# Counting relation ids as base-128 digits and batching the half-row operand products in a two-layer graph kernel

**Chip, cores, metric.** One core of one Trainium2 chip. The metric is the device time of one execution in microseconds (us), as the median of several executions. The core's span in a profile is some 2 us shorter than that time.

## The reference, cut to what matters

128 graphs of 64 nodes with 768 features, `adj` holding 0 or 1. Layer 0 is a relational graph layer in which `adj` serves both as adjacency and as relation ids; layer 1 is a gated attention layer that the change doesn't touch.

```python
h = relu(layernorm(x))                       # layer 0
ctx = (adj @ (h @ Wadj.T + badj)) / deg + (adj.T @ (h @ Wrev.T + brev)) / rdeg + h @ Wself.T + bself
agg  = einsum('bij,bijr->bir', adj, E[rels])             # rels is adj
ragg = einsum('bij,bijr->bir', adj.T, E[rels.T + 40])
x = x + ctx + agg @ Wr.T + ragg @ Wrr.T + bias terms
# layer 1 works on relu(layernorm(x)) and doesn't take part in the argument
```

Because only an id's count matters, the kernel counts for every node how often each of the ids 1 to 39 occurs in its row and in its column, and multiplies the counts with a table of 39 + 39 + 3 rows.

## The kernel before

The kernel has two stages, one for each layer. A stage walks over 32 pairs of tiles of 128 rows (two graphs a tile). In the first stage, TensorE computes the seven products of a Strassen-like scheme for a pair, in 67 steps; the preparation of the next pair is merged into these steps at stated positions:

```python
def count(p, k, d):                    # on VectorE, four times a pair
    eq = work.tile([P, NV, N], BF16, name="eq", bufs=1)
    nc.vector.tensor_tensor(eq, AB[p][:, k, d, None, :].to_broadcast([P, NV, N]), vals, op=OP.is_equal)
    nc.vector.tensor_reduce(CNT[p][:, k, d * NV : (d + 1) * NV], eq, AX.X, OP.add)
    ...
def operands(p, k, q):                 # on TensorE, six times a pair
    ps = pss.tile([P, GT, 512], F32, name="pb")          # two such PSUM buffers
    for i in range(2):
        for g in range(GT):            # one graph: 64 of the 128 rows
            s = slice(g * N, (g + 1) * N)
            nc.tensor.matmul(ps[:, g, i * 3 * N : (i + 1) * 3 * N], H0[t][s, kb * P : (kb + 1) * P],
                             rts[p % 2][s, k]..., start=True, stop=True)
    if k == 0:                         # evicted by ScalarE
        nc.scalar.copy(A1[p][:, q]..., pv); return
    nc.scalar.copy(A22..., pv[:, :, 3:])
    nc.vector.tensor_sub(S3..., A1..., pv[:, :, :3])     # evicted by VectorE
    nc.vector.tensor_add(S1..., A22..., pv[:, :, :3])    # S1 has one buffer
...
steps = [..., (10, lambda: count(p, 0, 0)), (15, lambda: count(p, 0, 1)), (39, lambda: sum2(p)),
         (44, lambda: count(p, 1, 0)), (49, lambda: count(p, 1, 1)),
         (46, lambda: count_t(p, 0)), (62, lambda: count_t(p, 1)), ...]
for q in range(KH):                    # KH = 3
    steps.append((20 + 3 * q, lambda q=q: operands(p, 0, q)))
    steps.append((30 + 4 * q, lambda q=q: operands(p, 1, q)))
```

The position sets an instruction's priority. The framework that builds the program fixes the order on each engine ahead of time, by its own estimate of what is ready when; an instruction with a late position may still be placed early, where the estimate sees its engine idle.

Of the kernel before, what the change touches and what calls it, by code (L numbers as in the profile page):

```python
# [8 lines left out]
F32 = mybir.dt.float32  # L9
BF16 = mybir.dt.bfloat16  # L10
I32 = mybir.dt.int32
AF = mybir.ActivationFunctionType
OP = mybir.AluOpType
AX = mybir.AxisListType

P = 128
# [6 lines left out]
def kernel(  # L23
# [48 lines left out]
    nc = tc.nc  # L72
    G, N, D = x.shape
    NREL = e_t.shape[1]
    NB = NREL // 2
    NV = NB - 1
    KB = D // P
    KH = KB // 2
# [4 lines left out]
    NP = NT // 2  # L83
    HALF = D // 2
    HH = H // 2
    NCNT = 2 * NV


    NROW = NCNT + 3
    PARTS = ((0, P // 3), (P // 3, NROW))  # L90
    W = DO + 1
    assert GT == 2 and N == 64 and DO == P and H == KB and KB % 2 == 0 and H % 2 == 0
    assert 3 * (NROW - P // 3) <= P and NT % 2 == 0 and HALF <= 512 and HH * W <= 512

# [57 lines left out]
    with ExitStack() as px:  # L152
        wa = px.enter_context(tc.tile_pool(name="wa", bufs=1))
        work = px.enter_context(tc.tile_pool(name="work0", bufs=2))
# [5 lines left out]
        def load(p):  # L160
            if p >= NP:
                return
            for t in (2 * p, 2 * p + 1):
                X[t] = work.tile([P, D], F32, name="x", bufs=6)
                nc.sync.dma_start(X[t], xf[t * P : (t + 1) * P, :])
            AI[p] = work.tile([P, 2, 2, N], I32, name="ai")
            for d, src in ((0, adj), (1, adj_t)):
                nc.sync.dma_start(
                    AI[p][:, :, d, :],
                    src[p * 2 * GT : (p + 1) * 2 * GT].rearrange("(t g) i j -> (g i) t j", g=GT))  # L170
# [23 lines left out]
        for i, v in enumerate((br, brr, badj, brev, bself)):  # L194
# [6 lines left out]
        blkb = wa.tile([P, P], BF16, name="blkb")  # L201
        nc.vector.tensor_copy(blkb, blk)

        vals = wa.tile([P, NV, N], BF16, name="vals")
        nc.gpsimd.iota(vals, pattern=[[1, NV], [0, N]], base=1, channel_multiplier=0,
                       allow_small_or_imprecise_dtypes=True)
        rts = []
        for i in range(2):
# [58 lines left out]
                                                   op0=OP.mult, op1=OP.add)  # L267
                nc.vector.tensor_copy(tab, u[:m])

        H0, ADF, AB, CNT, CT_T = {}, {}, {}, {}, {}  # L270
        A1, A22, S1, S2, S3, S4 = {}, {}, {}, {}, {}, {}

        def norm(t):
            to = small.tile([P, 2], F32, name="rn")
            stats(X[t], to)
            h = H0[t] = work.tile([P, D], F32, name="h0")
            nc.scalar.activation(h, X[t], AF.Relu, scale=to[:, 0:1], bias=to[:, 1:2])  # L277

        def prep(p):

            af = ADF[p] = work.tile([P, 2, 2, N], F32, name="af", bufs=1)
            nc.vector.tensor_copy(af, AI[p])
            AB[p] = work.tile([P, 2, 2, N], BF16, name="ab")
            nc.gpsimd.tensor_copy(AB[p], af)  # L284
            cnt = CNT[p] = work.tile([P, 2, NROW], BF16, name="cnt")
            dg = small.tile([P, 2, 2], F32, name="dg")
            nc.vector.tensor_reduce(dg, af, AX.X, OP.add)
            nc.vector.tensor_scalar(cnt[:, :, NCNT : NCNT + 2], dg, 1.0, None, op0=OP.min)
            nc.vector.memset(cnt[:, :, NCNT + 2 : NCNT + 3], 1.0)

        def prep_r(p):


            ds = pss.tile([P, 2, 512], F32, name="pb")[:, 0, : 4 * N].rearrange(
                "p (k d n) -> p k d n", k=2, d=2)
            nc.tensor.matmul(ds, blkb, AB[p], start=True, stop=True)
            rd = work.tile([P, 2, 2, N], F32, name="rd", bufs=1)
            nc.vector.tensor_scalar(rd, ds, 1.0, None, op0=OP.max)
            nc.vector.reciprocal(rd, rd)
            for d in range(2):  # L300
                nc.vector.tensor_mul(rts[p % 2][:, :, 1 - d, :], ADF[p][:, :, d, :], rd[:, :, d, :])

        def count(p, k, d):
            eq = work.tile([P, NV, N], BF16, name="eq", bufs=1)
            nc.vector.tensor_tensor(  # L305
                eq, AB[p][:, k, d, None, :].to_broadcast([P, NV, N]), vals, op=OP.is_equal)
            with nc.allow_low_precision(reason="whole numbers up to 64"):
                nc.vector.tensor_reduce(CNT[p][:, k, d * NV : (d + 1) * NV], eq, AX.X, OP.add)  # L308
            if d == 1:
                c3 = CT_T[p, k] = work.tile([P, NROW, 3], BF16, name="c3")  # L310
                nc.gpsimd.tensor_copy(c3, CNT[p][:, k, :, None].to_broadcast([P, NROW, 3]))

        def count_t(p, k):
            c3 = CT_T[p, k]
            pn = pss.tile([P, 2, 512], F32, name="pb")[:, 0, :P].bitcast(BF16).rearrange(
                "p (i n) -> p i n", i=2)
            cn = CT_T[p, k] = work.tile([P, 2, P], BF16, name="cntT", bufs=4)
            for i, (a, b) in enumerate(PARTS):
                nc.tensor.transpose(pn[: 3 * (b - a), i, :],  # L319
                                    c3[:, a:b, :].rearrange("p v c -> p (v c)"), identb)  # L320
                nc.scalar.copy(cn[: 3 * (b - a), i, :], pn[: 3 * (b - a), i, :])  # L321

        def operands(p, k, q):


            t = 2 * p + k
            ps = pss.tile([P, GT, 512], F32, name="pb")
            for i in range(2):
                kb = 2 * q + i
                for g in range(GT):  # L330
                    s = slice(g * N, (g + 1) * N)
                    nc.tensor.matmul(ps[:, g, i * 3 * N : (i + 1) * 3 * N],  # L332
                                     H0[t][s, kb * P : (kb + 1) * P],
                                     rts[p % 2][s, k].rearrange("p s n -> p (s n)"),
                                     start=True, stop=True)
            pv = ps[:, :, : 6 * N].rearrange("p g (x n) -> p g x n", n=N)

            def blocks(ap):
                return ap.rearrange("p s (g n) -> p g s n", g=GT)

            if k == 0:
                if q == 0:
                    A1[p] = work.tile([P, KH, 2, 3, P], F32, name="a1")
                nc.scalar.copy(A1[p][:, q].rearrange("p h s (g n) -> p g (h s) n", g=GT), pv)  # L344
                return
            if q == 0:
                A22[p] = work.tile([P, KH, 3, P], F32, name="a22")
                S1[p] = work.tile([P, KH, 3, P], F32, name="s1", bufs=1)
                S3[p] = work.tile([P, KH, 3, P], F32, name="s3")
            nc.scalar.copy(blocks(A22[p][:, q]), pv[:, :, 3:])  # L350
            nc.vector.tensor_sub(blocks(S3[p][:, q]), blocks(A1[p][:, q, 0]), pv[:, :, :3])
            nc.vector.tensor_add(blocks(S1[p][:, q]), blocks(A22[p][:, q]), pv[:, :, :3])

        def sum2(p):
            S2[p] = work.tile([P, KH, 3, P], F32, name="s2", bufs=1)
            for q in range(KH):
                nc.gpsimd.tensor_sub(S2[p][:, q], S1[p][:, q], A1[p][:, q, 0])  # L357

        def sum4(p):
            S4[p] = work.tile([P, KH, 3, P], F32, name="s4", bufs=1)  # L360
            for q in range(KH):
                nc.gpsimd.tensor_sub(S4[p][:, q], A1[p][:, q, 1], S2[p][:, q])
# [68 lines left out]
        def side(p):  # L431

            if p >= NP:
                return []
            steps = [(4, lambda: load(p + 1)),
                     (0, lambda: prep(p)),
                     (0, lambda: norm(2 * p)),
                     (0, lambda: norm(2 * p + 1)),
                     (6, lambda: prep_r(p)),
                     (10, lambda: count(p, 0, 0)),  # L440
                     (15, lambda: count(p, 0, 1)),
                     (39, lambda: sum2(p)),
                     (44, lambda: count(p, 1, 0)),
                     (49, lambda: count(p, 1, 1)),
                     (46, lambda: count_t(p, 0)),
                     (62, lambda: count_t(p, 1)),
                     (99, lambda: sum4(p))]
            for q in range(KH):
                steps.append((20 + 3 * q, lambda q=q: operands(p, 0, q)))
                steps.append((30 + 4 * q, lambda q=q: operands(p, 1, q)))  # L450
            return steps

        def sums_of_weights():
            for q in range(KH):
# [20 lines left out]
    with ExitStack() as px:  # L475
        wb = px.enter_context(tc.tile_pool(name="wb", bufs=1))
        work = px.enter_context(tc.tile_pool(name="work1", bufs=2))
# [84 lines left out]
        def main(p):  # L562
# [19 lines left out]
            def part(t, s, q):  # L582
                if s == 0:
                    return HS[t][:, q * HH : (q + 1) * HH, :DO]
                return Z[t][:, q * HALF : (q + 1) * HALF].rearrange("p (h o) -> p h o", h=HH)

# [230 lines left out]
```

## Time and profile before

| | before |
|---|---|
| time, median of 3 | 2788.27 us (2785.63 to 2789.57) |
| start, to 126 us | TensorE 61% busy |
| steady part of the first stage, 126 to 1617 us | TensorE 100%, VectorE 66% busy |
| one pair in the steady part | 48.75 us |

A row of the profile's groups reads: source line, engine, operation, output<-input names, shapes, number of instructions | busy us, mean ns of one | idle time of the engine just before them and what ended most of it. PE is TensorE, PEld its weight loader, DVE VectorE, ACT ScalarE, POOL GpSimd.

### The profile page before, as it was taken

How to read it: one execution, taken by the hardware profiler on the slowest of the kernel's cores; microseconds unless marked ns; L12 is line 12 of the kernel's file. 1: busy time of each engine (PE TensorE's matmuls, PEld its weight loads, DVE VectorE, ACT ScalarE, POOL GpSimd, SP SyncE). 2: the span in 40 equal slices, each digit the busy share in tenths (PEclk: the TensorE clock that was granted, in tenths of full speed). 3: DMA queues.
4: the chain of work that ended last, by engine and by line, in shares of the span. 5: the costliest groups of instructions: out<-in, count | busy, mean ns of one | idle time of the engine just before them, and what ended most of it. 6: DMA issues, size and time to landing. Idle time of an engine off the chain costs nothing.

```text
span 2786.5 us, 29364 instructions
## 1 busy us (share of the span) xinstructions
PE 2677.9 (96%) x10360; PEld 1605.5 (58%) x10360; DVE 2013.0 (72%) x3928; ACT 857.1 (31%) x1891; POOL 667.6 (24%) x703
## 2 busy tenths in 40 slices
PE   3999999999999999999999969999999999999996
PEld 2555555555555555555555536666666666666663
DVE  8975757667675766757576227888888888888887
ACT  1111112111111211111121104555555555555554
POOL 4422223232222323222222212111111111112220
PEclk8999999999999999999999989999999999999998
DMA  4111112121111212111120141222222222222211
GB/s 155 38 37 43 65 36 72 36 72 36 44 65 37 72 36 72 36 45 64 36 70 35 46 179 36 70 70 70 71 70 70 70 71 70 70 72 75 72 57 40
DMA packets 90596, 173.07 MB, mean 62 GB/s; under 512 B 32845, under 2 KB 40653, under 8 KB 90450
## 3 DMA queue, kind: packets, MB, share of 16 engines
q1 hardware_dynamic: 81432, 157.32, 16.8%
q10 hardware_dynamic: 9018, 13.89, 1.4%
q8 instruction: 82, 1.34, 0.2%
q14 instruction: 64, 0.52, 0.1%
HBM read 95.67 MB, written 75.50 MB: 61 GB/s over the span
## 4 chain that ended last, share of the span: by engine, by line
PE 72%; DVE 17%; ACT 6%; issue 3%; DMA 2%; POOL 0%; SPq 0%; ACTq 0%; DVEq 0%; POOLq 0%
PE pwa L376 20%; PE pwb L376 14%; PE pwd L376 7%; PE pwc L376 6%; PE pb L332 6%; PE pma L573 5%; PE pmc L573 5%; DVE no L651 4%; PE pmb L573 2%; DVE f L721 2%; ACT e L720 2%; DVE f L722 2%; DVE f L723 2%; DVE f L712 2%; PE ps L707 2%
## 5 line engine op out<-in xcount | busy, mean ns | idle before, releaser
L376 PE MATMUL pwa<-bwT,s 128*128 128x384 f32 x1152 | 401.5, 493 | 0.0
L308 DVE TENSOR_REDUCE cnt<-eq 128x39 bf16<-128x2496 bf16 x128 | 352.3, 2752 | 1.0
L376 PEld LDWEIGHTS pwa<-bwT,s 128*128 128x128 f32 x1152 | 210.7, 190 | 141.6 <-issue 19.4
L573 PE MATMUL pma<-bvT,s 128*128 128x384 f32 x768 | 289.1, 486 | 0.0
L393 DVE TENSOR_TENSOR x<-pwa,x 128x384 f32<-128x384 f32 x128 | 69.3, 542 | 248.3 <-PE pwa L376 173.8
L658 POOL TENSOR_TENSOR pr<-th,wsd 128x768 f32<-128x768 f32 x64 | 137.2, 2144 | 436.3 <-ACT th L647 223.6
L376 PE MATMUL pwb<-bwT,s 128*128 128x384 f32 x576 | 216.6, 505 | 0.0
L332 PE MATMUL pb<-r,h 64*128 64x192 f32 x1536 | 179.5, 354 | 31.4 <-ACT h L277 17.6
L332 PEld LDWEIGHTS pb<-r,h 64*128 64x128 f32 x1536 | 123.8, 190 | 139.4 <-issue 113.0
L376 PE MATMUL pwb<-bw,s 128*128 128x384 f32 x576 | 201.3, 492 | 0.0
L376 PE MATMUL pwd<-bwT,a 128*128 128x384 f32 x576 | 199.6, 492 | 0.0
L376 PE MATMUL pwa<-bw,a 128*128 128x384 f32 x576 | 197.0, 489 | 0.0
L344 ACT COPY a<-pb 128x768 f32<-128x768 f32 x96 | 76.6, 799 | 377.6 <-PE pb L332 377.6
L376 PE MATMUL pwc<-bw,a 128*128 128x384 f32 x576 | 191.0, 486 | 0.0
L357 POOL TENSOR_TENSOR s<-s,a 128x384 f32<-128x384 f32 x96 | 96.8, 1010 | 383.6 <-PE pwa L376 303.2
L305 DVE TENSOR_TENSOR eq<-ab,vals 128x2496 bf16<-128x2496 bf16 x128 | 184.6, 1443 | 3.4 <-POOL ab L284 2.2
L656 ACT ACTIVATE dg<-idc,sd 128x64 f32<-128x64 f32 x384 | 128.3, 344 | 126.9 <-DVE no L651 126.8
L321 ACT COPY cntT<-pb 126x128 bf16<-126x128 bf16 (+1 forms) x128 | 34.1, 266 | 430.2 <-PE pb L319 430.2
L573 PEld LDWEIGHTS pma<-bvT,s 128*128 128x128 f32 x768 | 131.4, 190 | 52.4
L651 DVE SCALAR_TENSOR_TENSOR no<-th,wsd 128x128 f32<-128x128 f32 x384 | 151.6, 395 | 5.6 <-ACT th L647 0.9
L376 PEld LDWEIGHTS pwc<-bw,a 128*128 128x128 f32 x576 | 109.4, 190 | 76.3
L376 PEld LDWEIGHTS pwd<-bwT,a 128*128 128x128 f32 x576 | 106.8, 190 | 75.0 <-issue 7.2
(139 smaller groups left out, 4592.8 us busy)
## 6 DMA issues: line engine op xcount, KB each, us to landing
h<-h SPq DMA_DIRECT2D x128, 384.0 KB, 2.3
x<-in_x_dram SPq DMA_DIRECT2D x64, 384.0 KB, 3.4
xh<-x SPq DMA_DIRECT2D x64, 384.0 KB, 2.8
x<-xh SPq DMA_DIRECT2D x64, 384.0 KB, 3.4
out_dram<-f SPq DMA_DIRECT2D x64, 384.0 KB, 2.6
ai<-in_adj_dram SPq DMA_DIRECT2D x64, 64.0 KB, 1.8
ai<-in_adj_t_dram SPq DMA_DIRECT2D x32, 64.0 KB, 4.5
bw<-in_wadj_t_dram ACTq DMA_DIRECT2D x3, 576.0 KB
```

Source lines behind the costliest of these rows:

```text
L305: nc.vector.tensor_tensor(eq, AB[p][:, k, d, None, :].to_broadcast([P, NV, N]), vals, op=OP.is_equal)
L308: nc.vector.tensor_reduce(CNT[p][:, k, d * NV : (d + 1) * NV], eq, AX.X, OP.add)
L332: nc.tensor.matmul(ps[:, g, i * 3 * N : (i + 1) * 3 * N], H0[t][s, kb * P : (kb + 1) * P], rts[p % 2][s, k].rearrange("p s n -> p (s n)"), ...
L344: nc.scalar.copy(A1[p][:, q].rearrange("p h s (g n) -> p g (h s) n", g=GT), pv)
L357: nc.gpsimd.tensor_sub(S2[p][:, q], S1[p][:, q], A1[p][:, q, 0])
L376: nc.tensor.matmul(bank[b][:, :HALF], a()[:, q, s, :], bw[w][:, q, s, :], start=(first and q == s == 0), stop=(q == KH - 1 and s == 2), sk ...
L393: nc.vector.tensor_add(v, bank[b][:, :HALF], v)
L573: nc.tensor.matmul(bank[b, s][:, :HALF], a[p][:, q, :], bw[w][:, q, s, :], start=(first and q == 0), stop=(q == KH - 1), skip_group_check= ...
L651: nc.vector.scalar_tensor_tensor(no, th[:, h, :], 1.0, wsd[:, 1, h * DO : (h + 1) * DO], op0=OP.mult, op1=OP.mult, accum_out=sd[:, 1, h : ...
L656: nc.scalar.activation(dg[:, h, :], idc, AF.Copy, scale=sd[:, 1, h : h + 1])
L658: nc.gpsimd.tensor_mul(pr, th, wsd[:, 0, :].rearrange("p (h o) -> p h o", h=H))
L707: nc.tensor.matmul(po[:, i, :], PT[t][:, h, :], HS[t][:, h, :], start=True, stop=True)
```

## The change

It does two things to the first stage. The 39 ids are folded to 13 groups; an id in the second or third group weighs 128 or 16384 in place of 1, so that one fp32 sum holds three counts of at most 64 as base-128 digits. And the six operand calls, which stood three or four steps apart, are put together two by two. Here is the diff cut to its core:

```diff
+            for i, o in enumerate(over):
+                nc.vector.tensor_scalar(o, ab, float((i + 1) * NG), None, op0=OP.is_gt)
+            nc.vector.tensor_scalar(wo, over[0], float(DIGIT - 1), 1.0, op0=OP.mult, op1=OP.add)
+            nc.vector.scalar_tensor_tensor(wo, over[1], ..., wo, op0=OP.mult, op1=OP.add)
+            nc.vector.scalar_tensor_tensor(gr, over[0], -float(NG), ab, op0=OP.mult, op1=OP.add)
+            nc.vector.scalar_tensor_tensor(gr, over[1], -float(NG), gr, op0=OP.mult, op1=OP.add)
...
-        def count(p, k, d):
-            eq = [P, NV, N]; is_equal; tensor_reduce            # cut: shown above
+        def count(p, k):
+            eq = work.tile([P, 2, NG, N], BF16, name="eq", bufs=1)
+            nc.vector.tensor_tensor(eq, GR[p][:, k, :, None, :]..., vals..., op=OP.is_equal)
+            nc.vector.tensor_tensor(eq, eq, WO[p][:, k, :, None, :]..., op=OP.mult)
+            nc.vector.tensor_reduce(SUM[p][:, k], eq, AX.X, OP.add)
+        def digits(p):
+            nc.vector.tensor_copy(si, SUM[p]...)                 # to int32
+            for i in range(3):
+                nc.vector.tensor_scalar(di[:, :, i, :], si, i * sh, DIGIT - 1,
+                                        op0=OP.logical_shift_right, op1=OP.bitwise_and)
+            nc.vector.tensor_copy(CNT[p][:, :, :NCNT]..., di...)
...
-                     operands(p, 0, q) at 20, 23, 26; operands(p, 1, q) at 30, 34, 38   # cut
+                    (10, lambda: count(p, 0)),
+                    (18, lambda: operands(p, 0, 0)),
+                    (18, lambda: operands(p, 0, 1)),
+                    (26, lambda: operands(p, 0, 2)),
+                    (26, lambda: operands(p, 1, 0)),
+                    (34, lambda: operands(p, 1, 1)),
+                    (34, lambda: operands(p, 1, 2)),
+                    (36, lambda: sum2(p)),
+                    (40, lambda: count(p, 1)),
+                    (46, lambda: digits(p)),
+                    (60, lambda: count_t(p, 0)),
+                    (60, lambda: count_t(p, 1)),
```

More of the change, by code (lines that the diff above doesn't have):

```diff
@@ L85 @@
     HH = H // 2
+    NG = NV // 3
+    DIGIT = 2 * N
     NCNT = 2 * NV
@@ L90 @@
     PARTS = ((0, P // 3), (P // 3, NROW))
+    assert NV == 3 * NG and DIGIT ** 3 <= 1 << 24
     W = DO + 1
@@ L202 @@
         nc.vector.tensor_copy(blkb, blk)
-        vals = wa.tile([P, NV, N], BF16, name="vals")
-        nc.gpsimd.iota(vals, pattern=[[1, NV], [0, N]], base=1, channel_multiplier=0,
+        vals = wa.tile([P, NG, N], BF16, name="vals")
+        nc.gpsimd.iota(vals, pattern=[[1, NG], [0, N]], base=1, channel_multiplier=0,
                        allow_small_or_imprecise_dtypes=True)
@@ L268, in build_table @@
                 nc.vector.tensor_copy(tab, u[:m])
-        H0, ADF, AB, CNT, CT_T = {}, {}, {}, {}, {}
+        H0, ADF, AB, CNT, CT_T, GR, WO, SUM = {}, {}, {}, {}, {}, {}, {}, {}
         A1, A22, S1, S2, S3, S4 = {}, {}, {}, {}, {}, {}
@@ L282, in prep @@
             nc.vector.tensor_copy(af, AI[p])
-            AB[p] = work.tile([P, 2, 2, N], BF16, name="ab")
-            nc.gpsimd.tensor_copy(AB[p], af)
+            ab = AB[p] = work.tile([P, 2, 2, N], BF16, name="ab")
+            nc.vector.tensor_copy(ab, af)
             cnt = CNT[p] = work.tile([P, 2, NROW], BF16, name="cnt")
@@ L289, in prep @@
             nc.vector.memset(cnt[:, :, NCNT + 2 : NCNT + 3], 1.0)
+            gr = GR[p] = work.tile([P, 2, 2, N], BF16, name="gr")
+            wo = WO[p] = work.tile([P, 2, 2, N], BF16, name="wo")
+            over = [work.tile([P, 2, 2, N], BF16, name=f"ov{i}", bufs=1) for i in range(2)]
+            for i, o in enumerate(over):
+                nc.vector.tensor_scalar(o, ab, float((i + 1) * NG), None, op0=OP.is_gt)
+            nc.vector.tensor_scalar(wo, over[0], float(DIGIT - 1), 1.0, op0=OP.mult, op1=OP.add)
+            nc.vector.scalar_tensor_tensor(wo, over[1], float(DIGIT * DIGIT - DIGIT), wo,
+                                           op0=OP.mult, op1=OP.add)
+            nc.vector.scalar_tensor_tensor(gr, over[0], -float(NG), ab, op0=OP.mult, op1=OP.add)
+            nc.vector.scalar_tensor_tensor(gr, over[1], -float(NG), gr, op0=OP.mult, op1=OP.add)
+            SUM[p] = work.tile([P, 2, 2, NG], F32, name="sum")
         def prep_r(p):
@@ L301, in prep_r @@
                 nc.vector.tensor_mul(rts[p % 2][:, :, 1 - d, :], ADF[p][:, :, d, :], rd[:, :, d, :])
-        def count(p, k, d):
-            eq = work.tile([P, NV, N], BF16, name="eq", bufs=1)
+        def count(p, k):
+            eq = work.tile([P, 2, NG, N], BF16, name="eq", bufs=1)
             nc.vector.tensor_tensor(
-                eq, AB[p][:, k, d, None, :].to_broadcast([P, NV, N]), vals, op=OP.is_equal)
-            with nc.allow_low_precision(reason="whole numbers up to 64"):
-                nc.vector.tensor_reduce(CNT[p][:, k, d * NV : (d + 1) * NV], eq, AX.X, OP.add)
-            if d == 1:
+                eq, GR[p][:, k, :, None, :].to_broadcast([P, 2, NG, N]),
+                vals[:, None, :, :].to_broadcast([P, 2, NG, N]), op=OP.is_equal)
+            nc.vector.tensor_tensor(
+                eq, eq, WO[p][:, k, :, None, :].to_broadcast([P, 2, NG, N]), op=OP.mult)
+            nc.vector.tensor_reduce(SUM[p][:, k], eq, AX.X, OP.add)
+        def digits(p):
+            si = work.tile([P, 4, NG], I32, name="si", bufs=1)
+            nc.vector.tensor_copy(si, SUM[p].rearrange("p k d v -> p (k d) v"))
+            di = work.tile([P, 4, 3, NG], I32, name="di", bufs=1)
+            sh = DIGIT.bit_length() - 1
+            for i in range(3):
+                nc.vector.tensor_scalar(di[:, :, i, :], si, i * sh, DIGIT - 1,
+                                        op0=OP.logical_shift_right, op1=OP.bitwise_and)
+            nc.vector.tensor_copy(
+                CNT[p][:, :, :NCNT].rearrange("p k (d v) -> p k d v", d=2),
+                di.rearrange("p (k d) i v -> p k d (i v)", k=2))
+            for k in range(2):
                 c3 = CT_T[p, k] = work.tile([P, NROW, 3], BF16, name="c3")
@@ L434, in side @@
                 return []
-            steps = [(4, lambda: load(p + 1)),
-                     (0, lambda: prep(p)),
-                     (0, lambda: norm(2 * p)),
-                     (0, lambda: norm(2 * p + 1)),
-                     (6, lambda: prep_r(p)),
-                     (10, lambda: count(p, 0, 0)),
-                     (15, lambda: count(p, 0, 1)),
-                     (39, lambda: sum2(p)),
-                     (44, lambda: count(p, 1, 0)),
-                     (49, lambda: count(p, 1, 1)),
-                     (46, lambda: count_t(p, 0)),
-                     (62, lambda: count_t(p, 1)),
-                     (99, lambda: sum4(p))]
-            for q in range(KH):
-                steps.append((20 + 3 * q, lambda q=q: operands(p, 0, q)))
-                steps.append((30 + 4 * q, lambda q=q: operands(p, 1, q)))
-            return steps
+            return [(4, lambda: load(p + 1)),
+                    (0, lambda: prep(p)),
+                    (0, lambda: norm(2 * p)),
+                    (0, lambda: norm(2 * p + 1)),
+                    (6, lambda: prep_r(p)),
+                    (10, lambda: count(p, 0)),
[10 more added lines that the diff above has]
+                    (60, lambda: count_t(p, 1)),
+                    (99, lambda: sum4(p))]
         def sums_of_weights():
```

## The prediction

> **What bounds the kernel now.** The kernel is two stages over 32 pairs of 128-row tiles. The first stage is the one that counts relation ids; the change touches nothing else. I read the page first, then a table of windows to split the stages.
>
> ```profile
> PE 2677.9 (96%) x10360; PEld 1605.5 (58%) x10360; DVE 2013.0 (72%) x3928; ACT 857.1 (31%) x1891; POOL 667.6 (24%) x703
> ```
>
> The averages mix the stages, so the windows (columns: busy time of each engine with its instructions, then granted clock):
>
> ```profile
> 0.00:126.00 126.00, 76.90 (x269) 44.11 (x270) 111.47 (x145) 18.12 (x29) 56.92 (x50) 0.89 0.26 87
> 126.00:1617.00 1491.00, 1491.00 (x5701) 862.30 (x5700) 988.31 (x1489) 260.94 (x420) 387.11 (x451) 1.00 0.15 51
> 1617.00:2786.00 1169.00, 1109.95 (x4394) 699.07 (x4392) 913.23 (x2295) 577.99 (x1442) 223.52 (x203) 0.98 0.22 74
> ```
>
> From 126 us to 1617 us TensorE is busy for 1491.00 of 1491.00 us at full clock; VectorE is busy for 66%. Only the first 126 us have TensorE idle, 49 us of it, and there VectorE is 88% busy. Next, the groups that the change removes or regroups:
>
> ```profile
> L308 DVE TENSOR_REDUCE cnt<-eq 128x39 bf16<-128x2496 bf16 x128 | 352.3, 2752 | 1.0
> L305 DVE TENSOR_TENSOR eq<-ab,vals 128x2496 bf16<-128x2496 bf16 x128 | 184.6, 1443 | 3.4 <-POOL ab L284 2.2
> L332 PE MATMUL pb<-r,h 64*128 64x192 f32 x1536 | 179.5, 354 | 31.4 <-ACT h L277 17.6
> ```
>
> Counting is 537 us of VectorE, the largest item there, but no TensorE group waits for it in the steady part. A busy TensorE is not a TensorE without loss, though, so I looked at start-to-start times, in the timeline of one pair:
>
> ```profile
> 819.32 0.81 PE L376 MATMUL pwb<-bwT,s 128*128 128x384 f32 x2
> 820.06 0.92 PE L332 MATMUL pb<-r,h 64*128 64x192 f32 x8
> 820.91 2.20 PE L376 MATMUL pwb<-bwT,s 128*128 128x384 f32 x6
> 823.04 0.92 PE L332 MATMUL pb<-r,h 64*128 64x192 f32 x8
> 823.90 2.20 PE L376 MATMUL pwb<-bwT,s 128*128 128x384 f32 x6
> 826.03 0.92 PE L332 MATMUL pb<-r,h 64*128 64x192 f32 x8
> ```
>
> Each fp32 product is two instructions in the trace. Undisturbed, 18 instructions of L376 take 5.80 us in the chain that ended last, 0.3224 us each. Here six of them take 823.04 - 820.91 = 2.13 us instead of 1.93: 0.20 us are lost around each group of half-row products (L332), about half on the way in (two take 0.74 instead of 0.645) and half on the way out. The group itself takes 0.85 us. The waits of the weight loader, asked for from 130 to 1590 us (30 pairs), say the same:
>
> ```profile
> PEld pb L332 <- issue: 98.1, 180, 0.5
> ```
>
> 180 is six groups in each of 30 pairs, one wait of 0.5 us per group: the loads of half-row weights do not get ahead of the full-array products before them.
>
> **What the Trainium skill says.** (1) "TensorEngine Tiling (Array Packing)", Tiling Modes: changing the tiling mode, not just the tile, drains the TensorE. The trace agrees: 0.20 us per group of 64-row products between 128-row ones. (2) "TensorE: Matmul & The Clock Gate", Part 3: a weight load overlaps running matmuls only where its row group differs. The trace's 180 waits fit. (3) "VectorE: DVE Perf Modes", the perf-mode tier table: tensor_tensor on bf16 runs at two elements a cycle, tensor_reduce at one. The trace agrees: 2496 elements in 1443 ns against 2752 ns; at the page's 0.96 GHz both leave a fixed part near 0.15 us.
>
> **The change part by part.** The positions at which side work is merged (18, 26, 34) count the 67 steps of a pair, most of them one product of two instructions. In the steady part TensorE's order follows them: the groups of L332 above stand three steps apart, as their positions 20, 23, 26 ask.
>
> Counting. Before, for each pair: 4 compares of 1443 ns and 4 sums of 2752 ns, 16.8 us. After: the ids are folded to 13 groups; for each half of the pair one compare over 2x13x64 = 1664 elements, one multiply by the weight 1, 128 or 16384, and one sum in fp32. Estimated from the two rows with their fixed parts: 1664/2/0.96 + 143 = 1.01 us twice and 1664/0.96 + 152 = 1.89 us once, 3.9 us a half, 7.8 us a pair. Added on VectorE: the cast of ids that leaves GpSimd (about 0.3 us, as L282's cast of 256 elements took 0.317), two comparisons and one multiply-add of 256 elements (0.2 each), three two-tensor multiply-adds of 256 (0.4 each, from L651's 395 ns for 128 and L721's 958 ns for 768), and the five small steps that take the digits apart (0.2 each, between L288's and L282's). That is 0.3 + 0.6 + 1.2 + 1.0 = 3.1 us. VectorE gives up 16.8 - 7.8 - 3.1 = 5.9 us a pair, 189 us in all: its total should fall from 2013 to about 1825 us. In the steady part this lies beside a full TensorE and is worth nothing.
>
> Operand products. The same 48 instructions a pair, but in three batches of 16 in place of six of 8. What a batch costs is seen where the prologue happened to run them together:
>
> ```profile
> 101.74 1.62 PE L332 MATMUL pb<-r,h 64*128 64x192 f32 x16 [0.24 <-ACT a L344]
> 103.56 0.92 PE L332 MATMUL pb<-r,h 64*128 64x192 f32 x8 [0.20 <-ACT a L344]
> ```
>
> The eight further instructions add 1.62 - 0.92 = 0.70 us, so a batch takes 0.85 + 0.70 = 1.55 us, and 0.20 for the two switches: 1.75, against 2 x (0.85 + 0.20) = 2.10 for two groups. Saved: 0.35 us a batch, 1.05 us a pair. Pair 0's operands are in the prologue, so 31 pairs: 32 us on the path that sets the end. As a check, 126 x 0.3224 + 6 x 1.05 + 8 products of counts (1.3) + four transposes and the sum of degrees (0.4) = 48.6 against a measured period of 48.75 us (844.28 - 795.52, the same group one pair apart); the new period should be 47.7.
>
> Prologue. TensorE waits 11.83 us there for L352 on VectorE, behind the counts of pair 0 and three sums of weights:
>
> ```profile
> 30.83 2.75 DVE L308 TENSOR_REDUCE cnt<-eq 128x39 bf16<-128x2496 bf16 x1
> ...
> 34.09 3.88 DVE L455 TENSOR_TENSOR bwT<-bwT,bw 128x1152 f32<-128x1152 f32 x3
> 37.90 3.88 DVE L457 TENSOR_TENSOR bwT<-bw,bwT 128x1152 f32<-128x1152 f32 x3
> 41.70 3.88 DVE L461 TENSOR_TENSOR bwT<-bw,bwT 128x1152 f32<-128x1152 f32 x3
> ```
>
> With 5.9 us less of counting the first sum could start near 28 us. The second needs the last weight block, whose transfer, in the chain, runs from 23.86 for 9.36 us, to 33.2. So that sum moves from 37.90 to no earlier than 33.2: 4.7 us at most. Later counting also holds up the tables (a sum of 2.75 us stands between their steps at 67.5 us). I give the prologue 6 us, with half as much either way.
>
> Sum: 2788.3 - 32 - 6 = 2750 us, 1.4% less.
>
> **The rivals.** (a) VectorE is the hidden limit, and its 189 us come off the time: about 2600 us. For it: 66% busy and counts that take 2.75 us at a time. Against it: no idle TensorE in 1491 us. I give this almost nothing. (b) The batching is given back as new waits. A batch takes both PSUM buffers of pb at once, and the middle batch, at step 26, writes S1, which has one buffer, before the last two steps that read the old S1 (26 and 27). The write waits for 4 x 0.3224 = 1.3 us after the batch, then 1.1 us for two evictions, perhaps a sum of 1.9 us ahead of them: up to 4.3 us, against 5.2 us (16 x 0.3224) until the next batch needs the buffer. It fits, by 0.9 us. If it does not, up to 1 us a pair is lost and the time is 2770 to 2785. (c) The loss is in each operand call and not in the switch, so batching saves nothing: only the prologue, 2782. The 0.70 against 0.92 speaks against it, but from one place in the trace. (d) A lighter VectorE shortens the prologue more than counted, as TensorE idles 49 us there and runs at a reduced clock: another 10 us, 2740.
>
> **Range and chances.** 2750 us; 8 times in 10 between 2736 and 2772. The low end is (d) with a batch a little cheaper than taken, the high end is (b) in part or (c) in part. To be over 2% faster it must be under 2733 us, 17 us beyond the sum: 0.07. Within 2%: 0.91. Over 2% slower needs a stall of 2.8 us in every pair: 0.02.
>
> **What would show it.** The weight loader's waits before L332 should go from 180 to about 90 in the same 30 pairs. The timeline should have operand groups of 16 that take near 1.55 us to the next start, and equal groups a pair apart should stand 47.7 us apart. VectorE should total about 1825 us with TensorE still without idle in the steady part, and the second stage should last as long as before, 1169 us from 1617 us on. It would be wrong if TensorE showed idle before L332 with S1 or the evictions as releaser, if groups of 16 were broken up by the schedule, or if the start moved by over 10 us.

## The result, and the profile after

The changed kernel takes 2748.93 us (median of 4, 2748.06 to 2749.11), the kernel before beside it 2788.14 us. The ratio is 0.986, with a 95% interval from 0.9843 to 0.9877.

The page's first line and the windows of the changed kernel (start, steady part, second stage):

```profile
PE 2631.0 (96%) x10360; PEld 1612.3 (59%) x10360; DVE 1819.3 (66%) x4248; ACT 844.1 (31%) x1891; POOL 635.7 (23%) x671
...
0.00:126.00 126.00, 72.41 (x274) 43.41 (x275) 96.34 (x179) 18.11 (x29) 41.74 (x49) 0.88 0.26 87
126.00:1580.00 1454.00, 1451.22 (x5704) 871.23 (x5704) 810.90 (x1775) 248.72 (x420) 369.73 (x420) 1.00 0.15 52
1580.00:2747.00 1167.00, 1107.38 (x4385) 697.67 (x4383) 912.08 (x2294) 577.28 (x1442) 224.22 (x203) 0.98 0.22 74
```

VectorE has lost 194 us, the time 39. TensorE's busy time has fallen by 47 us with the same 10360 instructions: some of what the profile counted as busy before was loss. The steady part now has 2.8 us of idle TensorE, which it did not have. The timeline of one pair (start, duration, engine, instructions) shows the batches:

```profile
806.56 1.57 PE L364 MATMUL pb<-r,h 64*128 64x192 f32 x16
808.06 1.56 PE L408 MATMUL pwb<-bwT,s 128*128 128x384 f32 x4
809.46 4.03 PE L408 MATMUL pwa<-bwT,s 128*128 128x384 f32 x12
813.42 1.57 PE L364 MATMUL pb<-r,h 64*128 64x192 f32 x16
814.92 2.20 PE L408 MATMUL pwa<-bwT,s 128*128 128x384 f32 x6
```

A batch takes 808.06 - 806.56 = 1.50 us to the next start. The four full-row instructions after it take 1.40 us in place of 4 x 0.3224 = 1.29 (0.11 lost on the way out), the twelve before the next batch 3.96 in place of 3.87 (0.09 on the way in). The weight loader's waits, from 130 to 1540 us:

```profile
PEld pb L364 <- issue: 51.3, 93, 0.8
```

These are 93 in 30 pairs, where there were 180. And the three large counting groups:

```profile
L327 DVE TENSOR_REDUCE sum<-eq 128x26 f32<-128x1664 bf16 x64 | 120.6, 1884 | 1.0
L325 DVE TENSOR_TENSOR eq<-eq,wo 128x1664 bf16<-128x1664 bf16 x64 | 65.0, 1016 | 0.1
L322 DVE TENSOR_TENSOR eq<-gr,vals 128x1664 bf16<-128x1664 bf16 x64 | 63.9, 999 | 0.6
```

To find where the 39.3 us of the two profiled spans (2786.5 and 2747.2) come from, I took fixed marks in both traces: the twelve full-row products that begin pair 1 (source line L376 before, L408 after the change), and the last count product of the stage.

| stretch | before | after | gained |
|---|---|---|---|
| to the start of pair 1 | 124.70 | 122.91 | 1.8 |
| pair 1 to the last count product | 1504.28 | 1466.44 | 37.8 |
| from there to the end | 1157.5 | 1157.9 | -0.4 |

In the middle stretch, 25 of the 30 spacings of pairs are 47.355 us, against 48.754 before: 1.40 us a pair, 42.0 us in 30. The other five are 48.12 to 48.32 us and give back 4.1 us.

One of these five, first on TensorE, then on VectorE:

```profile
384.81 0.92 PE L364 MATMUL pb<-r,h 64*128 64x192 f32 x8
386.24 0.92 PE L364 MATMUL pb<-r,h 64*128 64x192 f32 x8 [0.50 <-DVE s L384]
```

```profile
373.83 1.02 DVE L146 BATCH_NORM_STATS2 st<-x 128x6 f32<-128x384 f32 x2 [1.90 <-DMA x<-in_x_dram]
...
382.36 1.89 DVE L327 TENSOR_REDUCE sum<-eq 128x26 f32<-128x1664 bf16 x1
...
385.54 0.55 DVE L384 TENSOR_TENSOR s<-a,pb 128x384 f32<-128x384 f32 x1
```

VectorE sat for 1.90 us waiting for an input tile that came late. Everything behind it in its queue is late too. The last thing in that queue before the eviction L384 is counting, done for later use; the eviction ends at 386.1 us, and the second half of the third batch, which needs that PSUM buffer, had to wait for it. The batch falls apart and pays the switches as well. All five long pairs show the same: a wait of VectorE for an input tile of 1.90 to 2.09 us, and some 12 us later a wait of TensorE of 0.49 to 0.69 us, which add up to the 2.8 us of idle TensorE above.

In the prologue TensorE's first wait for an eviction is longer than before (18.70 us against 11.83), and a new one of 8.54 us stands behind it. TensorE, then VectorE's sums of weights:

```profile
52.93 1.65 PE L364 MATMUL pb<-r,h 64*128 64x192 f32 x8 [18.70 <-DVE s L384]
88.81 2.93 PE L364 MATMUL pb<-r,h 64*128 64x192 f32 x16 [8.54 <-ACT h L281]
```

```profile
24.99 4.04 DVE L488 TENSOR_TENSOR bwT<-bwT,bw 128x1152 f32<-128x1152 f32 x3 [0.36 <-DMA bw<-in_wadj_t_dram]
40.59 6.53 DVE L490 TENSOR_TENSOR bwT<-bw,bwT 128x1152 f32<-128x1152 f32 x3
47.04 3.88 DVE L494 TENSOR_TENSOR bwT<-bw,bwT 128x1152 f32<-128x1152 f32 x3
```

The first sum starts 9.1 us sooner than before, but the second 2.7 us later and it takes 6.53 us in place of 3.88. Between them VectorE did the preparation of pair 1. For the first 4 of the 6.53 us GpSimd's own sum of weights runs too, from 35.77 us on for 8.86 us.

### The profile page after: what moved, and what is told of

It is laid out like the page before. It is cut to its first block, busy times and chain, and to the rows that moved or that the text cites. A ratio compares the mean times of both kernels' runs of the same rounds, so it can differ in the third digit from the quotient of the medians.

```text
span 2747.2 us, 29590 instructions
## 1 busy us (share of the span) xinstructions
PE 2631.0 (96%) x10360; PEld 1612.3 (59%) x10360; DVE 1819.3 (66%) x4248; ACT 844.1 (31%) x1891; POOL 635.7 (23%) x671
## 4 chain that ended last, share of the span: by engine, by line
PE 68%; DVE 20%; ACT 6%; issue 3%; DMA 2%; POOL 1%; ACTq 0%; SPq 0%; DVEq 0%; POOLq 0%
PE pwa L408 20%; PE pwb L408 13%; PE pwd L408 7%; PE pwc L408 6%; PE pma L606 5%; PE pb L364 5%; PE pmc L606 5%; DVE no L684 4%; PE pmb L606 2%; DVE f L754 2%; ACT e L753 2%; DVE f L755 2%; DVE f L756 2%; DVE f L745 2%; PE ps L740 2%
## 5 line engine op out<-in xcount | busy, mean ns | idle before, releaser
L408 PE MATMUL pwa<-bwT,s 128*128 128x384 f32 x1152 | 390.3, 489 | 0.0
L408 PEld LDWEIGHTS pwa<-bwT,s 128*128 128x128 f32 x1152 | 215.4, 190 | 145.2 <-issue 7.0
L408 PE MATMUL pwb<-bw,s 128*128 128x384 f32 x576 | 201.5, 489 | 0.0
L364 PE MATMUL pb<-r,h 64*128 64x192 f32 x1536 | 156.5, 343 | 46.5 <-ACT h L281 25.0
L408 PE MATMUL pwb<-bwT,s 128*128 128x384 f32 x576 | 199.9, 492 | 0.0
L408 PE MATMUL pwa<-bw,a 128*128 128x384 f32 x576 | 197.5, 490 | 0.0
L408 PE MATMUL pwc<-bw,a 128*128 128x384 f32 x576 | 191.0, 486 | 0.0
L408 PE MATMUL pwd<-bwT,a 128*128 128x384 f32 x576 | 191.0, 486 | 0.0
L364 PEld LDWEIGHTS pb<-r,h 64*128 64x128 f32 x1536 | 126.3, 191 | 107.8 <-issue 71.7
L376 ACT COPY a<-pb 128x768 f32<-128x768 f32 x96 | 73.8, 801 | 367.8 <-PE pb L364 367.8
L353 ACT COPY cntT<-pb 117x128 bf16<-117x128 bf16 (+1 forms) x128 | 28.0, 269 | 491.0 <-PE pb L351 491.0
L408 PEld LDWEIGHTS pwc<-bw,a 128*128 128x128 f32 x576 | 109.4, 190 | 76.3
L408 PEld LDWEIGHTS pwd<-bwT,a 128*128 128x128 f32 x576 | 109.4, 190 | 76.3
L146 DVE BATCH_NORM_STATS2 st<-x 128x6 f32<-128x384 f32 x256 | 139.2, 554 | 22.2 <-DMA x<-in_x_dram 18.0
L408 PEld LDWEIGHTS pwa<-bw,a 128*128 128x128 f32 x576 | 106.4, 191 | 69.4 <-issue 9.1
```

Source lines behind the costliest of these rows:

```text
L146: nc.vector.bn_stats(st[:, i, :], src[:, i * HALF : (i + 1) * HALF])
L376: nc.scalar.copy(A1[p][:, q].rearrange("p h s (g n) -> p g (h s) n", g=GT), pv)
L408: nc.tensor.matmul(bank[b][:, :HALF], a()[:, q, s, :], bw[w][:, q, s, :], start=(first and q == s == 0), stop=(q == KH - 1 and s == 2), sk ...
```

## The experiments

Theory A: only the number of changes between full-row and half-row products counts on TensorE; VectorE's relief is hidden. The rivals are in the expectations. Twelve kernels ran, all with correct results. Times of the kernel before beside them: 2787.35, 2787.94 and 2787.36 us.

| label | median us | ratio | usual spacing of pairs, us |
|---|---|---|---|
| the change | 2748.93 | 0.986 | 47.36 |
| digits_only | 2784.7 | 0.999 | 48.64 (digits_again) |
| batch_only | 2776.77 | 0.996 | 48.0 to 48.9 |
| apart | 2782.33 | 0.9985 | 48.55 |
| split4 | 2860.73 | 1.0266 | 51.14 |
| batch_gate | 2751.97 | 0.9877 | 47.47 |
| after_gate | 2744.63 | 0.985 | 47.36 |
| batch_s1x2 | 2854.44 | 1.025 | 51.2 |
| batch_h1x1 | 2857.79 | 1.025 | 51.2 |
| weights_first | 2742.43 | 0.9839 | 47.36 |
| early_gate | 2735.29 | 0.9814 | 47.36 |
| beside_counts | 2734.36 | 0.981 | 47.22 |

### How the loss goes with the number of groups

split4 cuts each operand call of the kernel before into two groups of four instructions:

```diff
-                steps.append((20 + 3 * q, lambda q=q: operands(p, 0, q)))
-                steps.append((30 + 4 * q, lambda q=q: operands(p, 1, q)))
+                for i in range(2):
+                    steps.append((20 + 3 * q + i, lambda q=q, i=i: operands(p, 0, q, i)))
+                    steps.append((30 + 4 * q + i, lambda q=q, i=i: operands(p, 1, q, i)))
```

`sum2` moves from 39 to 40, behind the last half that it reads; a first build without that read memory not yet written and didn't run.

> The kernel before with each operand call cut into two halves of 4 instructions on two neighbouring steps: 12 groups of 4 a pair. Theory A (the loss is per group): six more groups at 0.35 to 0.42 us each, period 50.8 to 51.3 us, total 2850 to 2865 us, about 360 waits of the weight loader in 30 pairs. Rival D (the loss is per operand call or per PSUM tile, not per switch): 2788 us.

apart takes the changed kernel and moves the second call of each batch by one step:

```diff
-                    (18, lambda: operands(p, 0, 1)),
+                    (19, lambda: operands(p, 0, 1)),
-                    (26, lambda: operands(p, 1, 0)),
+                    (27, lambda: operands(p, 1, 0)),
-                    (34, lambda: operands(p, 1, 2)),
+                    (35, lambda: operands(p, 1, 2)),
```

> The changed kernel with the second operand call of each batch one step later, so six groups of 8 again, at nearly the same times. Theory A (the loss is per switch): 5 or 6 switches a pair back, period 48.3 to 48.6 us, total 2777 to 2788 us. Rival C (the gain comes from where in the pair the operands lie, not from their being together): period stays at 47.4, total 2749 us.

The weight loader's waits before L336 (split4, 130 to 1660 us) and before L364 (apart, 130 to 1580 us):

```profile
PEld pb L336 <- issue: 164.4, 301, 0.8
```

```profile
PEld pb L364 <- issue: 75.0, 150, 0.5
```

Six more groups a pair cost 51.14 - 48.75 = 2.39 us, 0.40 each. Three more groups in apart cost 48.55 - 47.36 = 1.19 us, 0.40 each again. Rivals C and D fall: one step of 0.65 us between two calls undoes the gain. The lines shown are 10 and 5 waits a pair, but the same answers list the others under ScalarE as releaser: 30 and 29 more before L336 in split4 (16.4 and 15.8 us), 30 more before L364 in apart (16.4 us). Together they are 360 and 180 in 30 pairs, 12 and 6 a pair as expected.

What in a switch costs the time stays open. The groups differ from the full-row products in their rows (64 against 128) and in their width (192 against 384 elements), and no run changes one alone. The row count can't be all of it: the way out into bf16 count products of full rows is nearly free (see beside_counts).

### Each part alone

digits_only is the changed kernel with the operand calls at their old positions:

```diff
-                    (18, lambda: operands(p, 0, 0)), (18, ... 0, 1), (26, ... 0, 2), (26, ... 1, 0), (34, ... 1, 1), (34, ... 1, 2), (36, lambda: sum2(p))
+                    (20, lambda: operands(p, 0, 0)), (23, ... 0, 1), (26, ... 0, 2), (30, ... 1, 0), (34, ... 1, 1), (38, ... 1, 2), (39, lambda: sum2(p))
```

> The changed kernel with its operand calls back at the six separate positions of the kernel before (20, 23, 26, 30, 34, 38), so the counting with digits alone. Theory A (only TensorE's switches between full-row and half-row products count, VectorE's relief is hidden): period 48.7 us a pair, total 2784 to 2789 us, VectorE near 1820 us busy. Rival B (the relief of VectorE carries part of the gain): 2770 us or less.

Four of the five executions took 2783.19 to 2784.77 us. The fifth, the one profiled, took 15137.2 us, with every matmul about five times as long as usual (2.37 us a mean L408 instruction, 0.49 us elsewhere) at a granted clock of 1.00. VectorE's busy time in it, 1751.3 us, was not longer than usual. It is left out; nothing here explains it. So the kernel was run again for its profile:

> digits_only once more, for a profile from an ordinary execution: period 48.65 to 48.75 us with six waits of the weight loader a pair, VectorE near 1820 us, 2783 to 2786 us.

It took 2784.47 us in one run, which lies within the four fast times of digits_only. VectorE was busy for 1821.6 us, 191 us less than before, and the time fell by 3 us. That is the spacing of 48.64 against 48.75. It lies at the transposes of counts, which the change puts together, right before count products: by the start-to-start times of the pairs shown by both traces, they and the edges around them take 0.28 us beyond the undisturbed products, against 0.39 before. Theory A holds for the counting: the ratio's interval for it, 0.9976 to 1.0004, includes 1.

batch_only is the kernel before with the operand calls in batches:

```diff
-            for q in range(KH):
-                steps.append((20 + 3 * q, lambda q=q: operands(p, 0, q)))
-                steps.append((30 + 4 * q, lambda q=q: operands(p, 1, q)))
+            for n, k, q in ((18, 0, 0), (18, 0, 1), (26, 0, 2), (26, 1, 0), (34, 1, 1), (34, 1, 2)):
+                steps.append((n, lambda k=k, q=q: operands(p, k, q)))
```

> The kernel before with its old counting, but the operand calls at 18, 18, 26, 26, 34, 34. Theory A: period 47.4 to 47.5 us, total 2745 to 2756 us, about 90 waits of the weight loader before half-row products in 30 pairs. Rival B (the batches need the lighter VectorE to empty the PSUM buffers in time): TensorE idles before the second half of batches with VectorE as releaser, about 1 us in most pairs, total 2770 to 2785 us.

It took 2776.77 us. Theory A's 2745 to 2756 us are missed and rival B's waits are there. TensorE's longest total of waits, and one pair on TensorE and on VectorE:

```profile
PE pb L332 <- DVE s L352: 30.9, 29, 12.8
```

```profile
828.57 0.92 PE L332 MATMUL pb<-r,h 64*128 64x192 f32 x8
829.96 0.92 PE L332 MATMUL pb<-r,h 64*128 64x192 f32 x8 [0.47 <-DVE s L352]
```

```profile
826.14 2.75 DVE L308 TENSOR_REDUCE cnt<-eq 128x39 bf16<-128x2496 bf16 x1
...
829.27 0.55 DVE L352 TENSOR_TENSOR s<-a,pb 128x384 f32<-128x384 f32 x1
```

Of the 29 waits, 27 come after 126 us: 16.2 us in all, the longest 2.1 us. So the parts do not add: 3 us and 11 us alone, 39 us together. The stall of the five pairs of the changed kernel is here in almost every pair: a sum of 2.75 us stands ahead of the eviction that frees the batch's PSUM buffer.

### Is it the amount of counting, or its place in the queue?

batch_gate keeps the old counting of 16.8 us a pair and puts that of the second half behind the first eviction into S1, by a false dependence: a zero worked out from S1 is added to the ids.

```diff
+            if k == 1 and p:
+                if d == 0:
+                    nc.vector.tensor_scalar(zero, S1[p][:, 0, 0, 0:1], 0.0, None, op0=OP.mult)
+                    nc.vector.tensor_scalar(AG[p], AB[p][:, 1], zero, None, op0=OP.add)
+                ids = AG[p][:, d, :]
```

> Batches of operands with the old counting, but the old counts of a pair's second half made to depend on the first eviction into S1 (a zero read from it is added to the ids), so that they queue behind that eviction on VectorE. Theory E (batch_only lost its gain because 4.2 us of counting stands ahead of the eviction in VectorE's queue): no wait of TensorE for VectorE in most pairs, period 47.4 to 47.5 us, total 2746 to 2756 us, with VectorE still near 2020 us busy. Rival F (what counts is the sum of VectorE's work, so that only lighter counting helps): total stays at 2770 us or more.

The first line of its page, and the loader's waits in 130 to 1540 us:

```profile
PE 2644.1 (96%) x10360; PEld 1617.6 (59%) x10360; DVE 2054.7 (75%) x3990; ACT 850.9 (31%) x1891; POOL 702.6 (26%) x703
```

```profile
PEld pb L340 <- issue: 49.0, 90, 0.5
```

It took 2751.97 us with all 30 spacings 47.46 or 47.47 us, with more work on VectorE than in any other kernel: 2054.7 us. The order in the queue was the cause, not the load. (The dependence also moved the first half's counts in the order; the edit can't tell which of the moves mattered, only that the eviction no longer stands behind counting.) Without any digits, the batching reaches the changed kernel's time to within 3 us. What it lacks lies in the prologue: pair 1 begins at 130.12 us there, against 122.91.

after_gate puts the same dependence into the changed kernel, on `GR` in place of `AB`.

> The changed kernel with the same dependence. Theory E: the five waits of 0.5 to 0.7 us before the third batch go, every period 47.36 us, total 2743 to 2747 us. Rival: the five long pairs come from the late input rows themselves and stay, 2749 us.

It took 2744.63 us. The intervals of the two ratios overlap (0.9836 to 0.9863 here), but the trace is plain: the five long spacings are gone, all are 47.35 or 47.36. The late input rows are still there: between 120 and 1600 us VectorE waited 30 times for them, 52.6 us in all and 3.3 us at most, more than in the changed kernel (15.9 us). They no longer cost anything, so the cause was late rows and the queue's order together.

The prediction had named the single buffer of S1 as the wait that could eat the gain. batch_s1x2 gives S1 a second buffer in batch_only; for room, the normalised output of the first stage (`h1`) gives up one of its two.

```diff
-                S1[p] = work.tile([P, KH, 3, P], F32, name="s1", bufs=1)
+                S1[p] = work.tile([P, KH, 3, P], F32, name="s1", bufs=2)
-                h = work.tile([P, D], F32, name="h1")
+                h = work.tile([P, D], F32, name="h1", bufs=1)
```

> batch_only with two buffers for S1 (room made by one buffer in place of two for the first stage's normalised output). My prediction named the single buffer of S1 as the wait that could eat the gain. If it is: the stalls of 0.5 us go, total near 2750 us. Theory E (the queue order on VectorE does it, and the count stands ahead of the eviction here as well): total stays at 2772 to 2780 us.

This run failed as an experiment: 2854.44 us, slower than either forecast, because of the buffer taken away. Its control has only the `h1` line of that edit:

> The control for batch_s1x2: batch_only with the one buffer for the normalised output, but one buffer for S1 as before. If the lost buffer alone made batch_s1x2 slow, this is at 2850 to 2860 us too, and S1's second buffer gained nothing. If it is near 2777 us, S1's second buffer itself did harm.

It took 2857.79 us (2855.41 to 2858.28, against 2851.57 to 2865.88), so the second buffer of S1 made no clear difference in that setting. More direct is batch_only's own trace, where VectorE's idle time before the write to S1 (L352) was 0.4 us in all:

```profile
  PE pwb L376: 0.4, 1
```

The wait for the old S1 is not what TensorE waited for. Nor did the single buffer alone make the framework place the counting ahead of the eviction: in batch_s1x2, with two buffers, a sum of 2.75 us (713.10 us) still stands there. Why one buffer of `h1` costs so much is seen among VectorE's waits in batch_h1x1:

```profile
DVE eq L305 <- POOL ab L284: 75.9, 30, 3.8
```

VectorE waits up to 3.8 us in each pair for the cast of ids on GpSimd, and its queue with the evictions is late by that. The trace shows the chain: with one buffer, ScalarE waits before writing the second tile's `h1` until the DMA has taken the first (79.5 us in 30 waits, none in batch_only); GpSimd's sum that reads `h1` is late by that, and the cast stands behind it. This is the same mechanism, driven from another engine.

### The prologue

weights_first lets the preparation of pair 1 wait for the last sum of weights, by the same trick:

```diff
+            if p == 1:
+                nc.vector.tensor_scalar(zero, bw["T4"][:, KH - 1, 0, 0:1], 0.0, None, op0=OP.mult)
+                nc.vector.tensor_scalar(af, AI[p], zero, None, op0=OP.add)
```

> The changed kernel with the preparation of pair 1 made to depend on the last sum of weights (a zero read from it is added), so that it no longer stands ahead of the sums on VectorE in the prologue. If that preparation is why the prologue gained nothing: TensorE's wait for the first evictions falls from 18.7 to 9 to 13 us, and the first stage starts its steady part 3 to 8 us sooner, total 2741 to 2746 us. If the table chain behind it sets the end of the prologue: the wait falls but the total stays at 2748 us.

It took 2742.43 us and reached pair 1 at 116.47 us in place of 122.91, as expected. But TensorE's wait fell only to 16.85 us, not to 9 to 13. The second sum of weights (VectorE) starts at 33.21 us, soon after the last block has come, and then runs beside GpSimd's own sum of weights (POOL):

```profile
33.21 10.39 DVE L495 TENSOR_TENSOR bwT<-bw,bwT 128x1152 f32<-128x1152 f32 x3
```

```profile
32.42 9.97 POOL L497 TENSOR_TENSOR bwT<-bw,bwT 128x1152 f32<-128x1152 f32 x3 [0.33 <-DMA bw<-in_wself_t_dram]
```

It takes 10.39 us where it took 3.88 in the kernel before. The Trainium skill says so on the page "SBUF — State Buffer", section Who interferes with whom: a VectorE instruction with two SBUF inputs contends with a GpSimd instruction that reads SBUF. This trace agrees; who blocks whom within these 10 us, it doesn't show. In the kernel before it was GpSimd that was slow: its same sum started 1.4 us after VectorE's first and took 17.75 us, while VectorE's three took 3.88 us each.

early_gate is after_gate with the table of relation rows built first, in buffers of its own (those of `h1`, idle in the prologue), so that pair 1's tiles don't wait for it.

```diff
-                v = work.tile([P, D], F32, name="tv", tag="h0")
-                u = work.tile([P, D], F32, name="tu", tag="h0")
+                v = work.tile([P, D], F32, name="tv", tag="h1")
+                u = work.tile([P, D], F32, name="tu", tag="h1")
...
+        build_table()
         for _, step in first[:-1]:
             step()
-        build_table()
         sums_of_weights()
```

> after_gate with the table of relation rows built first in the prologue, in buffers of its own, so that it lies in the time in which TensorE waits for the weights. If the prologue is bound by the order of work on VectorE and TensorE and not by the loads: it ends 15 to 25 us sooner, total 2720 to 2732 us. If it is bound by the weight loads: 2740 us or more.

It took 2735.29 us and reached pair 1 at 114.01 us, 8.3 us sooner than after_gate. The expected 15 to 25 us did not come: TensorE then waits in order for the table's own weights (20.21 us at the start, from a load) and for VectorE again. The total lies between the two forecasts: order was part of it, the loads another.

### A version faster than both kernels

beside_counts has the early tables and no dependence; the batches stand right before count products:

```diff
-                    operands at 18, 18, 26, 26, 34, 34; sum2 at 36; count(p, 1) at 40; digits at 46; count_t at 60, 60
+                    operands at 18, 18, 46, 46, 61, 61; sum2 at 62; count(p, 1) at 40; digits at 42; count_t at 53, 53
```

> The changed kernel with the tables built first, and the three batches at steps 18, 46 and 61, each right before a pair of bf16 count products, in place of 18, 26 and 34; no dependence added. In the changed kernel's trace only the first batch, which already stands there, had no loss on its way out. If that is a rule: two further exits of 0.10 us saved a pair, period 47.15 us, and no long pairs, since the evictions are far from the counting; total 2726 to 2732 us against 2735 us for early_gate. If not: 47.36 us and 2734 to 2737 us.

One of the moved batches on TensorE:

```profile
808.10 1.57 PE L364 MATMUL pb<-r,h 64*128 64x192 f32 x16
809.60 0.50 PE L417 MATMUL pwd<-tab,cntT 126*128 126x384 bf16 x2
809.94 4.03 PE L408 MATMUL pwa<-bwT,s 128*128 128x384 f32 x12
```

The two count products take 0.34 us after a batch (0.33 elsewhere), and the twelve products after them 3.87 us, their undisturbed time: the way out is free here. The spacing fell by 0.13 us to 47.22, not by the 0.21 of two exits, and there are no long pairs. The transposes of counts, which now stand with fp32 products on both sides, take back 0.06 us. The total of 2726 to 2732 us was missed: pair 1 begins at 115.80 us, 1.8 us later than in early_gate. At 2734.36 us the median is the lowest, 1 us below early_gate, which is within the ranges of the two. Whether it is over 2% faster than the kernel before stays unclear (interval 0.9795 to 0.9824).

## Why the prediction was right, point by point

The time (2748.93 against 2750) and the class are right. That the number fits to 1 us is luck: two errors of opposite sign, the gain in spacing was taken 11 us too small, and the prologue 5.6 us too large; with the 4.1 us lost to late evictions they nearly cancel.

- *TensorE bounds the steady part, and counting is hidden there.* Right: digits_only took 191 us off VectorE and 3 us off the time. Rival (a) is out.
- *The loss is per switch of full to half rows.* Right, and now shown by dose: 3, 6 and 12 groups a pair. Rival (c) is out. The prediction's point (2) of the skill fits the half-row loads only: full-row loads ran beside full-row products, whose rows are the same, all along (862.30 us of loading in 1491.00 us of busy TensorE). So differing rows alone do not tell which loads wait.
- *Saved: 0.35 us a batch, 1.05 us a pair, 32 us.* Too small. It measured 0.40 us a group and 1.40 us a pair. The mis-sized term is the batch: 1.50 us and not 1.55, since the one pair of batches in the prologue from which I took 0.70 for the second eight ran slower than they do in the steady part (1.62 against 1.57 us in duration). Two things were missed: the first batch stands before bf16 count products and has no way out to pay (0.1 us), and the transposes of counts are put together (0.11 us), which belongs to the digits and not to the batches. By start-to-start times six groups took 6.30 us a pair and three batches take 5.01; with the 0.11 that is the 1.40.
- *Prologue 6 us.* The step that failed. It gave 1.8 us, of which 1.4 belong to the first pair's own batches: 0.4 us. I had the freed VectorE start the sums of weights sooner. The first did, by 9.1 us; but the room was filled with pair 1's preparation, which stood ahead of the second sum (40.59 us in place of 37.90). weights_first and early_gate show that 6 and 8 us were to be had there.
- *Rival (b), given back as new waits.* I gave it a share of the high end. It happens in 5 of 30 pairs (4.1 us), and in nearly all pairs with the old counting. The prediction had named idle TensorE before L332 and batches broken up as signs of being wrong; in those five pairs both came. The place was right (the buffer of pb before the third batch). S1's single buffer, which I put first, is not what binds; the 1.9 us sum "perhaps ahead of" the eviction, which I put last, is.
- *Counting costs and VectorE's total.* 1.01 us twice and 1.89 us once were estimated; 0.999, 1.016 and 1.884 measured. Total 1825 against 1819.3. The 0.4 us for each two-tensor multiply-add was met too (0.416 to 0.417), partly by luck: a straight line through the two fp32 lines that it is taken from gives 0.51.
- *The parts add.* The prediction treated the counting as worth nothing in the steady part. It is so by itself, but with the batches it shortens what stands ahead of the evictions: batch_only gave 11 us, not 32. What I called hidden was the reason why the other part worked. Whether it is the shorter counts, their places or the cast that left GpSimd, no run separates.
- *Small slips.* "Only the first 126 us have TensorE idle" holds for the first stage; the second has 59 us of it. The stall that would make the kernel over 2% slower is, from the prediction's sum, (2844 - 2750) / 31 = 3.0 us a pair and not 2.8.

In the change's 39.3 us, then: 42 us from the steady spacing (some 39 from the batches, 3 from the transposes), 4 lost to late evictions, 2 from the time before pair 1.

## What to carry to other kernels

An engine that is busy all the time may still be losing time between its instructions: compare start-to-start times beside a change of tile shape with undisturbed ones, and put products of one shape together. When two parts of a change are proposed, ask whether one only makes room for the other; run each alone. And where a buffer is freed by an engine with time to spare, look at what stands ahead of that instruction in the engine's queue before making the engine's work lighter: moving the work was worth as much as shrinking it.

## What the Trainium skill lacked or had wrong

- "TensorEngine Tiling (Array Packing)", Tiling Modes, says that a change of mode drains the TensorE but gives no size. Here a group of 64-row products between 128-row fp32 products cost 0.40 us more than the same products within a longer group, 0.20 us of it at its two edges. It does not say either that the way out into a bf16 128-row product is nearly free (0.34 us for two count products against 0.33).
- "VectorE: DVE Perf Modes", perf-mode tier table, has no row for scalar_tensor_tensor, and no page gives its time on bf16: on 256 bf16 elements in SBUF it took 416 to 417 ns, where tensor_scalar took 219 ns. The rows it has agree (tensor_reduce 1884 ns and tensor_tensor 999 to 1016 ns for 1664 bf16 elements).
- No page has an execution like the one of 15137.2 us with a granted clock of 1.00 and matmuls five times as long.
